# Five PSUM banks, later additions and one more one-hot buffer in the list stage of a two-layer relational graph convolution

## The chip, the core and the metric

The kernel runs on one core of a Trainium2 chip. The core has a matrix engine (TensorE, PE in the profile, with its weight loads as PEld), VectorE (DVE), ScalarE (ACT), GpSimd (POOL) and SyncE (SP), which issues transfers. The metric is the device time of one execution in microseconds (us). The kernel before takes 3114.19 us, the median of three runs (3112.14 to 3119.51).

## What is computed

A graph has N = 12500 nodes with C = 128 features and E = 200000 edges sorted by target `dst`. Each edge has one of ten relations, the greatest of ten of its attributes. Two layers follow each other:

```python
def _rgcn_layer(x, src, dst, edge_type, w_rel, root, bias):
    seg = dst * NUM_REL + edge_type
    xs = x[src]
    sums = segment_sum(xs, seg, num_segments=N * NUM_REL)
    cnt = segment_sum(ones(seg.shape), seg, num_segments=N * NUM_REL)
    mean = (sums / maximum(cnt, 1.0)[:, None]).reshape(N, NUM_REL, -1)
    return einsum('nrd,rdo->no', mean, w_rel) + x @ root + bias

h = relu(_rgcn_layer(x, src, dst, edge_type, w_rel1, root1, b1))
out = layernorm(x + _rgcn_layer(h, src, dst, edge_type, w_rel2, root2, b2))
```

All of it is float32.

## The kernel before

**Tiles.** The edges are cut into 1563 tiles of 128. A tile's source rows are fetched by one indirect transfer, which GpSimd issues (`gathered`, L751). A one-hot matrix, 128 edges by relations times target nodes, is made on VectorE by comparing each edge's key with a table of column numbers (`ones`, L759 to L771), and multiplied by the edge's weight 1/count on ScalarE (`weighted`, L757). TensorE multiplies rows by one-hot into a PSUM tile `zp`; VectorE adds `zp` into a ring `cc` of sums by relation and node, at an offset that it reads from memory into a register (`offsets`, L777, and `sum_into`, L792). When all edges of a block of nodes are in, TensorE multiplies its sums by the ten relation matrices (`projected`, L739 and L742), and the block is finished.

**Layer 1** (L832 to L1013) walks through all tiles in groups of four. A tile whose targets lie late enough finds many of its sources already finished; a table `XH` then holds both the input row and the row after layer 1, so one gather serves both layers, and the second layer's part is added to the second ring at once.

**Layer 2** (`layer_2`, L1289 to L1521) does what is left, in two kinds of bunches. First come 42 *plain* bunches, the first T0 = 166 tiles, four a bunch, with twelve node columns. Meanwhile `brought_together` (L1058) collects all other edges whose source was not finished in layer 1 into a dense *list* of 695 tiles, by shifting the edges of each of 127 rows together. That is long work on VectorE, cut into steps between the plain bunches. Then come 476 *list* bunches of one to three tiles, from two walks taken in turns: walk 0 over the first part of the list adds into ring 1, walk 1 into ring 0. A list tile's targets span w = 14 to 119 nodes; a bunch has 10 x w columns a tile and at most 512 in all. A tile of more than 48 columns is worked in pieces that begin at column c = 0, 48 and 96, each a bunch of its own, with one gather for all of them.

**Order.** The program's order on each engine is written out by hand. Step p of layer 2's loop (L1451 to L1516) issues:

- the one-hots of bunch p + 4 (AH = 4), on VectorE, and the weights of bunch p + 3, on ScalarE;
- the gathers of bunch p and its products, on TensorE (L1480);
- due jobs, such as the next step of `brought_together`;
- the additions of bunch p - 2 (BE = 2), on VectorE. A plain bunch whose first tile is a multiple of 128 first has its row of offsets loaded from `b_i` by a transfer on ScalarE's queue (L1504), and VectorE reads it from there;
- the projection of a block whose last bunch was just added, and later steps that are due (`turn`, `norm`, `cleared`).

An engine waits where its next instruction needs a buffer or a value that is not there; everything behind waits too.

**Buffers.** Gathered rows lie in 7 buffers of eight tiles, so GpSimd may be at most 56 tiles ahead. There are 6 one-hot buffers (`OB`). PSUM has eight banks of 512 float32 a partition: two for blocks and transposes (`ps_f`), three for products (`ps_y`), and three for one tile `mask` (`ps_m`, L1051), which holds scratch of `brought_together` and, at the end, the tables of column numbers that the one-hots compare with: twelve columns for plain tiles, and three tables for the list, one for each c (L1170 to L1174), made from `wide` (L1083). The block's tiles `xb`, `fT`, `a`, `v` and `o` hold 512 float32 a partition.

Of the kernel before, what the change touches and what calls it, by code (L numbers as in the profile page):

```python
# [20 lines left out]
P = 128  # L21
NREL = 10
# [9 lines left out]
GB = 7  # L32
OB = 6
GQ = 8
# [30 lines left out]
def rgcn_resnorm_kernel(ctx: ExitStack, tc: tile.TileContext, x, src, dst, attr, w_rel1, root1, b1,  # L65
# [572 lines left out]
    def rows_in(k):  # L638

        last = "e" if k == len(ranges[-1]) - 1 else ""  # L640
        xb = fin.tile([P, len(block(k)[2]) if last else 4, C], F32, name="xb" + last)
        rows_dma(xb, x, k, False)
        return xb

    def features_in(k, l, xb):

        n0, n, subs = block(k)
        last = "e" if k == len(ranges[-1]) - 1 else ""
        fT = fin.tile([P, (len(subs) if last else 4) * P], F32, name="fT" + last)
# [17 lines left out]
    def shifted(po, k, l):  # L667

        n = block(k)[1]
        tail = {NBLK - 1: "e", NBLK - 2: "d"}.get(k, "")  # L670
        a = fin.tile([P, P if tail else YB], F32, name="a" + tail)
        nc.scalar.activation(a[:, :n], po[:, :n], AF.Identity if l else AF.Relu, bias=bsb[l])  # L672
        return a
# [19 lines left out]
    def normed(k, xb, pr):  # L693

        v = fin.tile([P, 4, C], F32, name="v")
        mv = small.tile([P, 4, 2], F32, name="mv")
# [11 lines left out]
        o = fin.tile([P, 4, C], F32, name="o")  # L708
        for t, h in subs:
# [48 lines left out]

    def ones(keys, cols, n, w):  # L759

        oh = dpool.tile([P, YB], F32, name="oh")
        m = NREL * w
        o = oh[:, :n * m]
        if w == WN:
            nc.vector.tensor_tensor(o.rearrange("p (t m) -> p t m", m=m), cols[:, None, :m].to_broadcast([P, n, m]),  # L765
                                    keys[:, :, None].to_broadcast([P, n, m]), op=ALU.is_equal)
        else:
            nc.vector.tensor_tensor(o.rearrange("p (t r n) -> p t r n", r=NREL, n=w),  # L768
                                    cols[:, None, :, :w].to_broadcast([P, n, NREL, w]),
                                    keys[:, :, None, None].to_broadcast([P, n, NREL, w]), op=ALU.is_equal)  # L770
        return oh  # L771
# [60 lines left out]
    def layer_1():  # L832
# [6 lines left out]
        def finish(k, t):  # L839
# [39 lines left out]
            def second_kept(_):  # L879
                n0, n, _ = block(k)  # L880
                p2 = po.pop()
                t2 = fin.tile([P, YB], F32, name="v")
                nc.scalar.activation(t2[:, :n], p2[:, :n], AF.Identity, bias=bsb[1])  # L883
                nc.sync.dma_start(T2[:, n0:n0 + n], t2[:, :n])
# [18 lines left out]
            if k + 1 < NBLK - 1:  # L903
# [10 lines left out]
                def turned_kept(t):  # L914
                    n0, n, subs = block(k + 1)
                    pt = po.pop()
                    fTs[k + 1] = fin.tile([P, 4 * P], F32, name="fT")
                    nc.scalar.activation(fTs[k + 1][:, :n], pt[:, :n], AF.Copy)
# [139 lines left out]
    def brought_together(ready, first):  # L1058
# [15 lines left out]
        for to, a, o in ((Si, src, 0), (A[:, P:], CN, 0), (K, KD, L)):  # L1074
# [3 lines left out]
            if whole < NR:  # L1078
                nc.sync.dma_start(to[whole:NR, :real], bass.AP(a.tensor, a.offset + o + (NT - RT) * P, [[ER, 1], [1, real]]))
        tri, wide = flat[:, at:at + P], flat[:, at + P:at + P + NREL * WZ].rearrange("p (r n) -> p r n", n=WZ)  # L1080
        assert at + P + NREL * WZ <= NREL * RW
# [87 lines left out]
        yield 1  # L1169
        for c in range(0, WMAX, WZ):  # L1170
            w = min(WZ, WMAX - c)
            t = mask[:, c * NREL:(c + w) * NREL].bitcast(F32).rearrange("p (r n) -> p r n", n=w)
            nc.vector.tensor_scalar(t, wide[:, :, :w], float(c), None, op0=ALU.add)
            tables[c, WZ] = t  # L1174
        assert WMAX * NREL <= ER
        n = -(-NT2 // P)
# [4 lines left out]
        def put(i, c):  # L1181
# [4 lines left out]
            assert m * P <= EW  # L1186
            o = WMAX * NREL + i * (EW // P)
            assert o + EW // P <= EW - KW
# [100 lines left out]
    def layer_2():  # L1289
# [90 lines left out]
        def fetched(k):  # L1380
# [4 lines left out]
            if k != partial:  # L1385
                assert k != final or partial in ended
                xbs[k] = (comp if tail else fin).tile([P, 4, C], F32, name="xb" + tail)
                rows_dma(xbs[k], x, k, False)
            fTs[k] = (comp if tail else fin).tile([P, 4 * P], F32, name="fT" + tail)
            nc.sync.dma_start(fTs[k][:, :n], T2[:, n0:n0 + n])  # L1390

        def finish(k, i):
# [19 lines left out]
            def turn(_):  # L1412
                a = fin.tile([P, YB], F32, name="a")
                nc.scalar.activation(a[:, :n], po.pop()[:, :n], AF.Copy)
# [29 lines left out]
        gs, ohs, zps, offs = {}, {}, {}, {}  # L1444
        AH, BE = 4, 2
        i = 0
# [243 lines left out]
```

## Time and profile before

| | |
|---|---|
| median of three runs | 3114.19 us |
| the profiled execution, its own time | 3108.35 us |
| its span, first to last instruction | 3106.5 us |
| TensorE busy | 2368.2 us (76%), 11861 instructions |
| VectorE busy | 2031.1 us (65%), 5465 instructions |
| ScalarE busy | 1301.6 us (42%), 3177 instructions |
| GpSimd busy | 2295.8 us (74%), 2436 instructions |
| granted TensorE clock, mean of the span | 0.840 |

Positions are us from the span's start. Layer 2's gathers begin at 1969.4; the plain stage reaches to about 2210, the list stage from there to the end. In a group's row stand line, engine, operation, tile written <- tiles read, shapes and count, then busy time and mean ns of one, then idle time of the engine just before such instructions and what ended it. In the timeline stand start, duration, the instruction and in brackets the idle time before it with its releaser. "issue" is waiting that the profile cannot put down to anything. A busy share alone says little here: an engine can be in every slice the one that others wait for and still show gaps between its instructions.

### The profile page before, as it was taken

Reading aid. Unit: us, or ns where it says so; the run is one execution under the profiler, and the core shown is the slowest. Engines: PE = TensorE matmul, PEld = TensorE weight load, DVE = VectorE, ACT = ScalarE, POOL = GpSimd, SP = SyncE. Lnnn points to the kernel's source line nnn. Section 1 sums busy time; section 2 is a strip of 40 time slices with the busy share of each in tenths; the row PEclk is TensorE's granted clock in tenths of the full one; section 3 lists DMA queues with packets and bytes.
Section 4 is the critical chain, followed back from the end, with each engine's and each line's share of the span. In section 5 each row is a group of like instructions: output and inputs, shape, how many; then the busy total and the mean of one; then the engine's idle time right before and its main releaser. Section 6 shows DMA issues by size and latency. Waiting matters only on the chain.

```text
span 3106.5 us, 42362 instructions
## 1 busy us (share of the span) xinstructions
PE 2368.2 (76%) x11861; PEld 1949.5 (63%) x11861; DVE 2031.1 (65%) x5465; ACT 1301.6 (42%) x3177; POOL 2295.8 (74%) x2436
## 2 busy tenths in 40 slices
PE   2768787888787878787878788546467777777887
PEld 1556677777776767676767677545445555555665
DVE  6764657665656767655646464597776676777766
ACT  3533443433333434333433333332434455555643
POOL 7777777777777777777777777677777777777772
PEclk8768888888888889888888888767788888998988
DMA  6874444444545454545454444322222222222221
GB/s 191 270 216 143 141 145 141 140 146 122 161 122 162 124 157 129 159 122 160 125 158 127 128 121 118 95 59 62 64 67 68 72 73 74 72 73 73 79 73 43
DMA packets 265199, 370.97 MB, mean 119 GB/s; under 512 B 51232, under 2 KB 197189, under 8 KB 264958
## 3 DMA queue, kind: packets, MB, share of 16 engines
q0 software_dynamic: 99920, 250.57, 29.4%
q1 hardware_dynamic: 111347, 91.97, 9.4%
q10 hardware_dynamic: 53691, 25.62, 2.8%
q8 instruction: 102, 1.67, 0.2%
q14 instruction: 139, 1.14, 0.1%
HBM read 322.86 MB, written 57.89 MB: 123 GB/s over the span
## 4 chain that ended last, share of the span: by engine, by line
PE 30%; POOL 22%; issue 19%; DVE 14%; DMA 10%; ACT 2%; DVEq 1%; ACTq 0%; POOLq 0%; SPq 0%
POOL g L751 22%; PE pf L739 13%; DMA g<-XH,idxE 9%; PE zp L978 8%; PE zp L1480 6%; DVE cc L792 5%; DVE oh L768 2%; PE pf L742 1%; DVE cc L1158 1%; DVEq L777 1%; ACT cc L722 1%; ACT oh L757 1%; DVE oh L765 1%; DVE st L703 1%; DVE go L1146 1%
## 5 line engine op out<-in xcount | busy, mean ns | idle before, releaser
L751 POOL DMA_INDIRECT g<-XH,idxE x1397 | 1321.2, 946 | 425.6 <-issue 384.8
L792 DVE TENSOR_TENSOR cc<-cc,zp 128x240 f32 (+13 forms) x2500 | 959.8, 384 | 777.8 <-PE zp L978 388.2
L978 PE MATMUL zp<-oh,g 128*128 128x120 f32 x5920 | 983.2, 318 | 370.5 <-DMA g<-XH,idxE 206.8
L978 PEld LDWEIGHTS zp<-oh,g 128*128 128x128 f32 x5920 | 866.5, 222 | 487.2 <-issue 184.8
L751 POOL DMA_INDIRECT g<-hD,idxB x695 | 657.3, 946 | 215.9 <-issue 195.3
L739 PE MATMUL pf<-cc,w 128*128 128x256 f32 (+4 forms) x3000 | 732.1, 405 | 18.9 <-DVE cc L792 15.1
L1480 PE MATMUL zp<-oh,g 128*128 128x120 f32 (+23 forms) x1874 | 507.3, 415 | 284.4 <-DVE cc L792 156.4
L739 PEld LDWEIGHTS pf<-cc,w 128*128 128x128 f32 x3000 | 610.4, 215 | 121.1 <-DVE cc L792 22.5
L1480 PEld LDWEIGHTS zp<-oh,g 128*128 128x128 f32 x1874 | 338.9, 227 | 430.9 <-issue 271.0
L757 ACT ACTIVATE oh<-oh,wE 128x120 f32<-128x120 f32 x1729 | 530.9, 383 | 186.0 <-DVE oh L765 139.4
L757 ACT ACTIVATE oh<-oh,wB 128x150 f32<-128x150 f32 (+23 forms) x771 | 339.1, 482 | 296.5 <-DVE oh L768 269.4
L722 ACT ACTIVATE cc<-zero 128x1280 f32<-128x1280 f32 (+3 forms) x274 | 336.6, 1231 | 85.3 <-DVE cc L792 81.5
L768 DVE TENSOR_TENSOR oh<-go,keyB 128x480 f32<-128x480 f32 (+20 forms) x476 | 260.3, 547 | 115.1 <-PE zp L1480 113.6
L672 ACT ACTIVATE a<-pf,b 128x256 f32<-128x256 f32 (+1 forms) x50 | 23.3, 465 | 580.6 <-PE pf L742 578.9
L765 DVE TENSOR_TENSOR oh<-bank,keyE 128x480 f32<-128x480 f32 x391 | 253.0, 647 | 0.0
L751 POOL DMA_INDIRECT g<-hD,idxE x166 | 158.8, 957 | 61.7 <-issue 46.0
L751 POOL DMA_INDIRECT g<-in_x_dram,idxE x166 | 156.9, 945 | 52.2 <-issue 47.9
L883 ACT ACTIVATE v<-pf,b 128x256 f32<-128x256 f32 (+2 forms) x52 | 23.9, 459 | 361.4 <-PE pf L742 333.2
L548 DVE TENSOR_TENSOR eqb<-bank,kh 128x1344 bf16<-128x1344 f32 (+2 forms) x65 | 100.4, 1549 | 2.4 <-PE pf L559 2.0
L557 PE MATMUL pf<-eqb,identb 128*128 128x512 bf16 (+2 forms) x130 | 58.9, 453 | 12.4 <-DVE eqb L548 12.4
L559 PE MATMUL pf<-eqb,identb 128*128 128x512 bf16 (+2 forms) x130 | 58.5, 450 | 0.0
L706 ACT ACTIVATE rstd<-mv,eps 128x2 f32<-128x2 f32 (+5 forms) x54 | 15.9, 295 | 83.8 <-DVE mv L704 83.3
(235 smaller groups left out, 1097.8 us busy)
## 6 DMA issues: line engine op xcount, KB each, us to landing
m<-in_edge_attr_dram SPq DMA_DIRECT2D x48, 672.0 KB
g<-XH,idxE POOLq DMA_INDIRECT x1397
XH<-in_x_dram ACTq DMA_DIRECT2D x24, 512.0 KB
XH<-zero ACTq DMA_DIRECT2D x24, 512.0 KB
XH<-hb SPq DMA_DIRECT2D x87, 128.0 KB
g<-hD,idxB POOLq DMA_INDIRECT x695
xb<-in_x_dram SPq DMA_DIRECT2D x72, 128.0 KB
out_dram<-o SPq DMA_DIRECT2D x47, 128.0 KB
```

The source lines that it names most:

```text
L548: nc.vector.tensor_tensor(eq[:p], kpP[:p, None, :R].to_broadcast([p, DB, R]), fore, op=ALU.is_equal)
L557: nc.tensor.matmul(pc[:p], identb[:p, :p], eq[:p, k:k + 4, L:], start=(d + k == 1), stop=False)
L559: nc.tensor.matmul(pc[:p], identb[:p, :p], back, start=False, stop=(d + k + 3 == L))
L722: nc.scalar.activation(cc[:, l, h * H:(h + 1) * H, o:o + n], zero[:, None, :n].to_broadcast([P, H, n]), AF.Copy)
L739: nc.tensor.matmul(po[:, :n], wsb[l][:, r, :], cc[:, l if ring is None else ring, r, o:o + n], start=(r == 0), stop=False)
L751: nc.gpsimd.indirect_dma_start(out=g[:, j * C:(j + n) * C], out_offset=None, in_=table, in_offset=bass.IndirectOffsetOnAxis(ap=idx, axis=0))
L757: nc.scalar.activation(s, s, AF.Copy, scale=w)
L765: nc.vector.tensor_tensor(o.rearrange("p (t m) -> p t m", m=m), cols[:, None, :m].to_broadcast([P, n, m]), keys[:, :, None].to_broadcast([ ...
L768: nc.vector.tensor_tensor(o.rearrange("p (t r n) -> p t r n", r=NREL, n=w), cols[:, None, :, :w].to_broadcast([P, n, NREL, w]), keys[:, :, ...
L792: nc.vector.tensor_tensor(s, s, z, op=ALU.add)
L978: nc.tensor.matmul(zp[:, a + l * KW:a + (l + 1) * KW], g[:, (slot[j] + l) * C:(slot[j] + l + 1) * C], oh[:, j * KW:(j + 1) * KW], start=Tr ...
L1480: nc.tensor.matmul(zp[:, j * m:(j + 1) * m], gt[:, b * C:(b + 1) * C], oh[:, j * m:(j + 1) * m], start=True, stop=True)
```

## The change

Layer 2's list bunches get five PSUM banks in place of three. The tile `mask` is given back once the first list one-hots are due (`masking.close()` at p = plain - 4), and its three banks become the table `wide` and two product tiles `zq3` and `zq4`; bunch p takes one of `ps_y`'s three when p % 5 is 0, 1 or 2, and one of the two else. Only one table is left; a piece that begins at c = 48 or 96 adds c to it in the comparison. Additions come three bunches behind for list bunches, two for plain ones, as before. There are seven one-hot buffers, and the block's tiles shrink from 512 to 384 float32. The offsets of all plain tiles are loaded by two transfers on SyncE's queue when layer 2 begins, ahead of the loads of `brought_together`.

```diff
-OB = 6
+OB = 7
...
-        xb = fin.tile([P, len(block(k)[2]) if last else 4, C], F32, name="xb" + last)
+        xb = fin.tile([P, len(block(k)[2]) if last else 3, C], F32, name="xb" + last)
...
-    def ones(keys, cols, n, w):
+    def ones(keys, cols, n, w, c=0):
...
-            nc.vector.tensor_tensor(o.rearrange("p (t r n) -> p t r n", r=NREL, n=w),
-                                    cols[:, None, :, :w].to_broadcast([P, n, NREL, w]),
-                                    keys[:, :, None, None].to_broadcast([P, n, NREL, w]), op=ALU.is_equal)
+            to = o.rearrange("p (t r n) -> p t r n", r=NREL, n=w)
+            a = cols[:, None, :, :w].to_broadcast([P, n, NREL, w])
+            b = keys[:, :, None, None].to_broadcast([P, n, NREL, w])
+            if c:
+                assert n == 1
+                nc.vector.scalar_tensor_tensor(to[:, 0], a[:, 0], float(c), b[:, 0], op0=ALU.add, op1=ALU.is_equal)
+            else:
+                nc.vector.tensor_tensor(to, a, b, op=ALU.is_equal)
...
-    ps_m = fast.enter_context(tc.tile_pool(name="ps_m", bufs=1, space=PSUM))
     ps_y = fast.enter_context(tc.tile_pool(name="ps_y", bufs=3, space=PSUM))
+    masking = ExitStack()
+    ps_m = masking.enter_context(tc.tile_pool(name="ps_m", bufs=1, space=PSUM))
...
-        nc.vector.tensor_tensor(wide, spread[:, :, None].to_broadcast([P, NREL, WZ]),
-                                columns[:, None, :WZ].to_broadcast([P, NREL, WZ]), op=ALU.add)
...
-        for c in range(0, WMAX, WZ):
-            w = min(WZ, WMAX - c)
-            t = mask[:, c * NREL:(c + w) * NREL].bitcast(F32).rearrange("p (r n) -> p r n", n=w)
-            nc.vector.tensor_scalar(t, wide[:, :, :w], float(c), None, op0=ALU.add)
-            tables[c, WZ] = t
...
-        AH, BE = 4, 2
+        AH, BE = 4, 3
+        plain = sum(not b[1] for b in bunches)
+        rowP = comp.tile([1, -(-T0 // CT) * CT], I32, name="rowP")
+        for c in range(-(-T0 // CT)):
+            nc.sync.dma_start(rowP[:, c * CT:(c + 1) * CT], b_i[c:c + 1, :])
...
+            if p == plain - AH:
+                assert wanted[0] in ready
+                masking.close()
+                ps_n = fast.enter_context(tc.tile_pool(name="ps_n", bufs=1, space=PSUM))
+                tables[WZ] = ps_n.tile([P, NREL, WZ], F32, name="wide")
+                nc.vector.tensor_tensor(tables[WZ], spread[:, :, None].to_broadcast([P, NREL, WZ]),
+                                        columns[:, None, :WZ].to_broadcast([P, NREL, WZ]), op=ALU.add)
...
-                ohs[p + AH] = ones(keys[:, t0:t0 + n], tables[(c, WZ) if second else WN], n, w)
+                ohs[p + AH] = ones(keys[:, t0:t0 + n], tables[WZ if second else WN], n, w, c)
...
+            five = p >= plain
...
-                zp = zps[p] = ps_y.tile([P, YB], F32, name="zp")
+                if p % 5 > 2 and five:
+                    zp = ps_n.tile([P, YB], F32, name=f"zq{p % 5}")
+                else:
+                    zp = ps_y.tile([P, YB], F32, name="zp")
+                zps[p] = zp
...
-            q = p - BE
-            if q >= 0:
+            q = p - (BE if five else BE - 1)
+            if q in zps:
...
-                            if t % CT == 0:
-                                row = rows_.tile([1, CT], I32, name="row")
-                                nc.scalar.dma_start(row, b_i[t // CT:t // CT + 1, :])
-                            vals = offsets(row[:, t % CT:t % CT + m], t, m, bounds)
+                            vals = offsets(rowP[:, t:t + m], t, m, bounds)
```

More of the change, by code (lines that the diff above doesn't have):

```diff
@@ L648, in features_in @@
         last = "e" if k == len(ranges[-1]) - 1 else ""
-        fT = fin.tile([P, (len(subs) if last else 4) * P], F32, name="fT" + last)
+        fT = fin.tile([P, (len(subs) if last else 3) * P], F32, name="fT" + last)
         if l:
@@ L670, in shifted @@
         tail = {NBLK - 1: "e", NBLK - 2: "d"}.get(k, "")
-        a = fin.tile([P, P if tail else YB], F32, name="a" + tail)
+        a = fin.tile([P, P if tail else 3 * P], F32, name="a" + tail)
         nc.scalar.activation(a[:, :n], po[:, :n], AF.Identity if l else AF.Relu, bias=bsb[l])
@@ L693, in normed @@
     def normed(k, xb, pr):
-        v = fin.tile([P, 4, C], F32, name="v")
+        v = fin.tile([P, 3, C], F32, name="v")
         mv = small.tile([P, 4, 2], F32, name="mv")
@@ L707, in normed @@
             nc.vector.reciprocal(rstd[:p, s], rstd[:p, s])
-        o = fin.tile([P, 4, C], F32, name="o")
+        o = fin.tile([P, 3, C], F32, name="o")
         for t, h in subs:
@@ L881, in second_kept @@
                 p2 = po.pop()
-                t2 = fin.tile([P, YB], F32, name="v")
+                t2 = fin.tile([P, 3 * P], F32, name="v")
                 nc.scalar.activation(t2[:, :n], p2[:, :n], AF.Identity, bias=bsb[1])
@@ L916, in turned_kept @@
                     pt = po.pop()
-                    fTs[k + 1] = fin.tile([P, 4 * P], F32, name="fT")
+                    fTs[k + 1] = fin.tile([P, 3 * P], F32, name="fT")
                     nc.scalar.activation(fTs[k + 1][:, :n], pt[:, :n], AF.Copy)
@@ L1079, in brought_together @@
                 nc.sync.dma_start(to[whole:NR, :real], bass.AP(a.tensor, a.offset + o + (NT - RT) * P, [[ER, 1], [1, real]]))
[L1080 to L1081 removed]
+        tri = flat[:, at:at + P]
+        assert at + P <= NREL * RW
         yield 1
[L1083 to L1084 removed]
         nc.vector.memset(below, 1.0)
@@ L1186, in put @@
             assert m * P <= EW
-            o = WMAX * NREL + i * (EW // P)
+            o = i * (EW // P)
             assert o + EW // P <= EW - KW
@@ L1386, in fetched @@
                 assert k != final or partial in ended
-                xbs[k] = (comp if tail else fin).tile([P, 4, C], F32, name="xb" + tail)
+                xbs[k] = (comp if tail else fin).tile([P, 3, C], F32, name="xb" + tail)
                 rows_dma(xbs[k], x, k, False)
-            fTs[k] = (comp if tail else fin).tile([P, 4 * P], F32, name="fT" + tail)
+            fTs[k] = (comp if tail else fin).tile([P, 3 * P], F32, name="fT" + tail)
             nc.sync.dma_start(fTs[k][:, :n], T2[:, n0:n0 + n])
@@ L1412, in turn @@
             def turn(_):
-                a = fin.tile([P, YB], F32, name="a")
+                a = fin.tile([P, 3 * P], F32, name="a")
                 nc.scalar.activation(a[:, :n], po.pop()[:, :n], AF.Copy)
```

1 line of the change is left out of this document (removed).

## The prediction

> **What bounds the kernel now.** I read the page first, for the engine that is never idle for long.
>
> ```profile
> span 3106.5 us, 42362 instructions
> ...
> POOL 7777777777777777777777777677777777777772
> ...
> L751 POOL DMA_INDIRECT g<-hD,idxB x695 | 657.3, 946 | 215.9 <-issue 195.3 <-PE zp L1480 14.2 <-DMA g<-hD,idxB 4.3
> ```
>
> GpSimd issues one gather of 128 rows after another, in every slice but the last. Each takes 946 ns and has about 0.3 us of "issue" behind it. So I asked for the gathers of layer 2 alone, by stretches (length, busy time of GpSimd, number, clock, DMA), and then for the timeline.
>
> ```profile
> 1969.40:3051.90 1082.50, 816.18 (x861) 0.84 0.28 71
> ...
> 1969.40:2210.50 241.10, 182.84 (x192) 0.69 0.28 70
> 1969.40:2481.70 512.30, 387.31 (x408) 0.76 0.27 69
> ```
>
> ```profile
> 2210.54 1.74 PE L1480 MATMUL zp<-oh,g 128*128 128x140 f32 x6 [0.45 <-ACT oh L757]
> ...
> 2479.86 0.95 POOL L751 DMA_INDIRECT g<-hD,idxB  x1 [0.30 <-issue]
> 2482.81 0.94 POOL L751 DMA_INDIRECT g<-hD,idxB  x1 [2.01 <-PE zp L1480]
> ...
> 3050.91 0.94 POOL L751 DMA_INDIRECT g<-hD,idxB  x1 [0.30 <-issue]
> ```
>
> Undisturbed, a gather starts every 1.25 us (0.95 + 0.30). The 861 gathers of layer 2 took 1082.5 us, or 1.257 each, so GpSimd hardly ever stood still. It ended at 3050.91 + 0.94 = 3051.85, and the kernel 54.6 us later. Those 54.6 us are what a faster pipeline behind the gathers can win.
>
> How far the products lag can be counted. The first product of the list starts at 2210.54; 192 gathers were issued by then and 166 of them are plain tiles, so the lag is 26 tiles. At 2482.81 gather 409 waits for a product: 408 is 51 buffers of eight, the next needs the 45th back, hence tile 360 was just used, a lag of 48. The last tile's gather starts at 3050.91 and its product at 3089.70, 38.8 us or 31 tiles later. So from 2205 to 3085 compute is about as fast as the gathers and drags a backlog along, and the backlog is what is paid after 3051.85. What holds it back there, by the view of waits (who waited for whom: total, times, longest):
>
> ```profile
> PE zp L1480 <- DVE cc L792: 113.7, 66, 7.4
> DVE oh L768 <- PE zp L1480: 113.6, 46, 5.4
> PE zp L1480 <- issue: 45.9, 20, 4.1
> DVE cc L792 <- PE pf L739: 35.6, 7, 6.6
> POOL g L751 <- PE zp L1480: 13.9, 32, 2.3
> ```
>
> TensorE and VectorE wait for each other. A typical case from the timeline:
>
> ```profile
> 2617.92 4.50 PE L739 MATMUL pf<-cc,w 128*128 128x256 f32 x20
> 2619.69 0.26 DVE L792 TENSOR_TENSOR cc<-cc,zp 128x110 f32 x1
> ...
> 2622.68 1.99 PE L1480 MATMUL zp<-oh,g 128*128 128x160 f32 x10
> 2623.77 0.66 DVE L768 TENSOR_TENSOR oh<-go,keyB 128x480 f32<-128x480 f32 x1 [3.82 <-PE zp L1480]
> ```
>
> While TensorE projects a block (L739), VectorE finishes the two bunches it has, then wants the one-hot buffer of a product that stands behind the projection, and idles 3.82 us. Then TensorE in turn finds its three banks full.
>
> **The change, part by part.** *Five banks, additions three behind, seven one-hots.* With three banks product p needs the addition of p-3; with six one-hots, ones(p+4) needs product p-2. So three bunches are in flight. Afterwards product p needs the addition of p-5 and ones(p+4) product p-3: five in flight. At a projection VectorE has one bunch more to do, and TensorE may run two further ahead. What one bunch of VectorE is worth:
>
> ```profile
> L792 DVE TENSOR_TENSOR cc<-cc,zp 128x150 f32 (+22 forms) x787 | 308.3, 392 | 104.6 <-PE pf L739 35.6 <-issue 31.6 <-ACT cc L722 12.0
> ...
> L768 DVE TENSOR_TENSOR oh<-go,keyB 128x480 f32<-128x480 f32 (+24 forms) x474 | 259.2, 547 | 115.1 <-PE zp L1480 113.6
> ```
>
> 0.547 us for the one-hot and 787/474 x 0.392 = 0.65 us of additions, 1.2 us together. Over the 46 waits of VectorE that is at most 55 us of compute time. The lower bound is nothing: where the next addition goes to the ring that the projection reads, it waits for the projection itself (the 35.6 us above), whatever the banks. I take 45 to 55, since only 7 waits are of that kind.
>
> How much is needed? The first list product will start about 9 us earlier (below), near 2201.5, and gathers allow the last one near 3050. That is 848 us for the 695 tiles against 3090.3 - 2210.5 = 880 now, 32 us less. 32 of 45 to 55 is enough, so I expect compute to catch up before the end, and **the last gather to set the end**. Anything saved beyond that changes nothing.
>
> *Offsets of the plain tiles, loaded at once; tables.* The rows of the plain stage:
>
> ```profile
> 1993.17 0.91 DVE L792 TENSOR_TENSOR cc<-cc,zp 128x120 f32 x3 [5.42 <-DMA row<-b_i]
> ...
> 2131.99 1.80 DVE L1173 TENSOR_SCALAR go<-cc 128x480 f32<-128x480 f32 x3
> ...
> 2179.97 1.22 DVE L792 TENSOR_TENSOR cc<-cc,zp 128x120 f32 x4 [9.37 <-DMA row<-b_i]
> ...
> 2172.78 4.49 PE L1196 MATMUL pf<-cc 127*128 127x256 f32 x20
> 2181.30 1.34 PE L1480 MATMUL zp<-oh,g 128*128 128x120 f32 x8 [4.03 <-issue]
> ...
> 1975.89 0.38 SPq L1390 DMA_DIRECT2D fTe<-T  x1
> ...
> L777 DVEq TENSOR_LOAD <-row x21: 593/598/829, 1992.3 to 2213.7; - x21
> ```
>
> The first wait of 5.42 us shrinks to the register load of about 0.6: 4.8 won. Two loads more on SP, at 0.38 each by the row of another load there, push the list's source rows behind them back 0.8. Net 4.0. The three tables (1.80 us) go away while VectorE sets the pace, 1.8 won; one table comes back as one addition of 480 columns, 0.66 on VectorE at the end of the stage by the one-hot of that size above. The second row wait is 9.37 on VectorE, but TensorE was busy with L1196 until 2177.27 and then stood 4.03: 4.0 won. Sum 4.0 + 1.8 + 4.0 - 0.66 = 9 us, all of it backlog.
>
> *Shifted one-hots.* A list tile wider than 48 columns is worked in pieces. The 771 - 695 = 76 later pieces get their one-hot from one instruction with two operations in place of a plain comparison with a ready table:
>
> ```profile
> L757 ACT ACTIVATE oh<-oh,wB 128x150 f32<-128x150 f32 (+23 forms) x771 | 339.1, 482 | 296.5 <-DVE oh L768 269.4 <-PE zp L1480 12.0 <-DVE dn L1254 9.9
> ...
> L1192 DVE TENSOR_TENSOR cc<-columns,go 127x1536 f32<-127x1536 f32 x1 | 1.8, 1753 | 0.0
> L1168 DVE SCALAR_TENSOR_TENSOR cc<-cc 127x1536 f32<-127x1536 int32 x1 | 1.8, 1752 | 0.0
> ```
>
> Over 1536 columns both forms take 1.75 us, so I price it at nothing. The bound above is a second pass over the columns, 76 x 0.66 = 50 us of VectorE at most; no row suggests it.
>
> *Smaller tiles of the blocks* move nothing: no block here is wider than 280 columns, and 384 are left.
>
> **The sum**, against the profiled execution (span 3106.5, time 3108.35). GpSimd no longer waits for buffers: 13.9 - 32 x 0.30 = 4.3 us, so its last gather ends at 3047.6. The first gather of the layer waits for layer 1, which is untouched. Then:
>
> ```profile
> 2191.36 2.24 DMA g<-hD,idxB
> ```
>
> ```profile
> 3084.51 4.88 PE L739 MATMUL pf<-cc,w 128*128 128x280 f32 x20
> 3089.23 0.64 PE L742 MATMUL pf<-fT,ident 128*128 128x280 f32 x2
> 3089.70 0.58 PE L1480 MATMUL zp<-oh,g 128*128 128x250 f32 x2
> ...
> 3090.80 4.64 PE L739 MATMUL pf<-cc,w 128*128 128x260 f32 x20
> ```
>
> The chain has 2.24 us from the end of a gather to the work on its rows; with 2.3 the last ones are there at 3049.9. The last block but one is complete three bunches before the end, and its projection is issued one bunch later than now, so behind the last product: product 0.6, projection 3084.51 to 3089.87, 5.4, then 0.9 until the last projection, and from there to the end 3106.5 - 3090.8 = 15.7. Together 22.6, end at 3072.5, a gain of 34. I allow 1 us for a remaining lag: 33. The median of the runs (3114.19) lies 5.8 above the profiled one, so I forecast 3114 - 33 = **3081 us**, own range 3073 to 3092.
>
> **The rivals.** *Compute stays behind.* If additions after a projection mostly meet the ring that it reads, the third bunch of cover is not to be had, and only the 9 us and perhaps a third of the 45 remain: gain 9 to 24, 3090 to 3105, at 14 us 3100. For it: that wait exists (35.6 us), and grows as the others shrink. Against: 46 waits to 7.
>
> *TensorE becomes the bound, by its clock.* Once paced by gathers, TensorE has more gaps, and the granted clock may fall:
>
> ```profile
> 200.00:1950.00 1750.00, 1440.44 (x8018) 1247.61 (x8016) 1069.78 (x2841) 680.63 (x1768) 1323.48 (x1401) 0.85 0.48 139
> 2000.00:2150.00 150.00, 74.29 (x307) 63.39 (x307) 136.04 (x246) 40.12 (x113) 113.53 (x120) 0.62 0.23 59
> 2205.00:3085.00 880.00, 670.68 (x2631) 487.82 (x2630) 627.98 (x1791) 448.74 (x938) 637.50 (x674) 0.88 0.27 71
> ```
>
> The columns are TensorE, weight loads, VectorE, ScalarE and GpSimd, then the clock. TensorE is busy 670.7 us of the list stage at 0.88. Of its 209 us idle, 113.7 + 45.9 are the ones in question, about 50 stay. At clock c it needs 670.7 x 0.88/c + 50, more than today's 880 below c = 0.71. The stage of 2000 to 2150 ran at 0.62 with TensorE half idle, so this is possible; at 0.68 the stage takes 918, 38 more than now, less the 9 gained before: 3143 us, slower. Against it: layer 1 is paced by gathers all along and holds 0.85.
> The Trainium skill, "TensorE: Matmul & The Clock Gate", section "A second HAM failure mode: psum-queue depth-cycling", speaks for this rival: a kernel that cycled through PSUM banks idled TensorE briefly between groups often enough that the clock swung between half and full. The 0.62 of that stage agrees with it, the 0.85 of layer 1 does not.
>
> *The change does not do what it says*: the two-operation one-hot costs its second pass, up to 50 us on VectorE, and eats the 45 to 55. Then 3105 to 3118, no change to speak of.
>
> **How the numbers follow.** Forecast 0.70, compute stays behind 0.19, second pass 0.04, clock 0.07. The range, 3073 to 3104, takes the forecast's own range and nearly all of the first rival; what is outside is the last two and some of the edges. A measurement here tells 0.2%, 6 us, from no change. Faster: 0.70 + 0.18 = 0.88; same 0.05; slower 0.07.
>
> **What would show it.** Right: the last gather starts near 3047 and no wait of GpSimd for a product is over 0.5 us; TensorE's waits for gathers appear among the list's products, and the wait on L792 falls under half of 113.7; the last product comes within 3 us of the last landing; no row load waits on VectorE. Wrong: a product of the last tile over 10 us behind its gather (compute stays behind: look for L792 waiting on L739), a clock under 0.75 in the list stage, or a one-hot of 480 columns with two operations at over 0.8 us.

## The result and the profile after

| | before | after |
|---|---|---|
| median of the runs beside each other | 3113.22 us (3110.39 to 3119.51) | 3086.33 us (3084.58 to 3086.88) |
| ratio, 95% interval | | 0.991 (0.9895 to 0.9924) |
| span of the profiled execution | 3106.5 us | 3084.8 us |
| granted TensorE clock, mean of the span | 0.840 | 0.834 |

The change makes the kernel 27 us faster. Forecast was 3081 us, with a range of 3073 to 3104. First the gathers of layer 2 in the changed kernel, in one stretch (length, busy time of GpSimd, number, clock, DMA share, GB/s):

```profile
1970.00:3048.90 1078.90, 816.72 (x861) 0.83 0.28 73
```

Then GpSimd's waits from 1969 to 3060 (who waited for whom: total, times, longest):

```profile
POOL g L751 <- PE pf L742: 12.6, 3, 12.0
POOL g L751 <- PE zp L1494: 7.0, 23, 0.3
...
POOL g L751 <- PE zq L1494: 1.8, 6, 0.3
```

Apart from the 12.0 us at the layer's first gather (11.4 before), no wait for a product is longer than 0.3 us, where the longest was 2.3. The full ring is gone. The last gather ends at 3048.87 (its row is in the timeline below), against 3051.85, though the first began 0.6 us later.

TensorE's and VectorE's waits in the list stage, 2195 to 3065:

```profile
DVE cc L797 <- PE pf L739: 48.4, 9, 10.1
PE zp L1494 <- DVE cc L797: 43.5, 24, 9.0
...
DVE oh L775 <- PE zp L1494: 34.1, 15, 5.9
DVE oh L775 <- PE zq L1494: 28.7, 11, 5.8
PE pf L739 <- DVE cc L797: 28.2, 16, 5.6
...
PE zq L1494 <- DVE cc L797: 21.4, 15, 3.8
...
DVE oh L773 <- PE zp L1494: 13.2, 7, 3.9
```

L1494 is the product of before's L1480, L797 the addition (L792), L775 the one-hot (L768), L773 the one-hot of a later piece. In the same window of the kernel before, TensorE waits 122.9 us for additions that free a bank and VectorE 110.0 us for products; after, these are 64.9 (zp and zq together) and about 77 (with L773). From 2205 to 3085, the window of the prediction's rows, TensorE's went from 113.7 to 55.9. The waits of additions for a projection that reads their ring grew from 35.6 to 48.4, and projections now wait 28.2 us for additions (7.2 before).

What ends the waits of TensorE late in the list, 2700 to 3053, after and then before:

```profile
PE zp L1494 <- DMA g<-hD,idxB: 14.6, 23, 1.5
PE zq L1494 <- DVE cc L797: 12.9, 9, 2.7
PE zq L1494 <- DMA g<-hD,idxB: 10.5, 16, 1.4
```

```profile
PE zp L1480 <- DVE cc L792: 33.3, 27, 3.4
...
PE zp L1480 <- DMA g<-hD,idxB: 2.4, 2, 1.8
```

Products now wait for rows (25.1 us, 39 times), before they hardly did (2.4). The backlog can be counted at any product: gathers begun by then, less the tiles of the bunches ahead of it. Each cell gives tiles and the position in us; "run" is from bunch 48 to bunch 324, all list bunches. The last three rows are experiments told below.

| kernel | bunch 48 | bunch 180 | bunch 324 | bunch 480 | run |
|---|---|---|---|---|---|
| before | 29 at 2236.7 | 49 at 2481.7 | 41 at 2730.1 | 31 at 3005.3 | 493.4 |
| after | 19 at 2224.5 | 37 at 2465.9 | 9 at 2685.4 | 5 at 2968.5 | 460.9 |
| banks alone | 28 at 2234.1 | 49 at 2479.9 | 34 at 2716.5 | 16 at 2982.3 | 482.4 |
| before, fewer additions | 29 at 2237.9 | 49 at 2482.3 | 30 at 2714.2 | 4 at 2969.5 | 476.3 |
| after, fewer additions | 19 at 2224.1 | 38 at 2465.8 | 8 at 2684.1 | 5 at 2968.1 | 460.0 |

The changed kernel runs 32.5 us faster between bunches 48 and 324 and stands 2 to 14 tiles behind the gathers from then on. So the backlog of 31 tiles is gone, and yet the span is only 21.7 us shorter. The rest was given back at the end. The timeline of the changed kernel from its last gather (start, duration, instruction, in brackets the idle time before it with its releaser):

```profile
3044.72 0.87 SPq L634 DMA_DIRECT2D out_dram<-o  x2
...
3047.93 0.94 POOL L751 DMA_INDIRECT g<-hD,idxB  x1 [0.30 <-issue]
...
3052.94 1.17 PE L1494 MATMUL zp<-oh,g 128*128 128x250 f32 x2 [0.46 <-DMA g<-hD,idxB]
...
3053.90 6.21 PE L739 MATMUL pf<-cc,w 128*128 128x280 f32 x20
...
3061.72 0.61 DVE L700 TENSOR_TENSOR v<-pf,xb 128x256 f32<-128x256 f32 x2 [11.48 <-PE pf L1419]
...
3063.99 0.85 DVE L710 TENSOR_SCALAR o<-v,mv,rstd 128x128 f32<-128x128 f32 x3
...
3064.76 2.31 DVE L797 TENSOR_TENSOR cc<-cc,zp 128x250 f32 x5
3067.13 6.16 PE L739 MATMUL pf<-cc,w 128*128 128x260 f32 x20 [5.45 <-DVE cc L797]
```

VectorE stands idle 11.48 us until the last block but one has been projected and turned round, normalizes it (L700 to L710), and only then adds the last five tiles, which the last projection waits for. TensorE stands 5.45 us. Both projections are also longer than before's (4.88 and 4.64). The windows of the two projections with the clock (length, then busy time and count of TensorE, weight loads, VectorE, ScalarE, GpSimd, then clock, DMA share, GB/s), after and before:

```profile
3053.90:3060.10 6.20, 6.20 (x22) 4.84 (x21) 0.00 (x0) 0.00 (x0) 0.00 (x0) 0.78 0.00 0
...
3067.10:3073.30 6.20, 6.17 (x21) 5.16 (x22) 0.00 (x0) 0.00 (x0) 0.00 (x0) 0.75 0.01 3
```

```profile
3084.51:3089.30 4.79, 4.79 (x22) 3.88 (x21) 1.06 (x3) 0.00 (x0) 0.00 (x0) 1.00 0.02 3
3090.80:3095.40 4.60, 4.60 (x23) 4.02 (x22) 2.81 (x13) 0.59 (x2) 0.00 (x0) 1.00 0.12 33
```

### The profile page after: what moved, and what is told of

Its sections match the earlier page's. It is cut to its first block, busy times and chain, and to the rows that moved or that the text cites. A ratio compares the mean times of both kernels' runs of the same rounds, so it can differ in the third digit from the quotient of the medians.

```text
span 3084.8 us, 42354 instructions
## 1 busy us (share of the span) xinstructions
PE 2376.9 (77%) x11861; PEld 1961.6 (64%) x11861; DVE 2025.7 (66%) x5462; ACT 1299.9 (42%) x3177; POOL 2296.4 (74%) x2436
## 4 chain that ended last, share of the span: by engine, by line
PE 29%; POOL 21%; issue 18%; DVE 15%; DMA 12%; ACT 2%; DVEq 1%; ACTq 0%; SPq 0%; POOLq 0%
POOL g L751 21%; PE pf L739 14%; PE zp L983 10%; DMA g<-XH,idxE 9%; DVE cc L797 5%; DVE oh L775 2%; PE zp L1494 1%; DMA g<-hD,idxB 1%; PE pf L742 1%; DVE cc L1162 1%; PE zq L1494 1%; DVE oh L765 1%; DMA g<-in_x_dram,idxE 1%; DVEq L782 1%; DVE go L1150 1%
## 5 line engine op out<-in xcount | busy, mean ns | idle before, releaser
L797 DVE TENSOR_TENSOR cc<-cc,zp 128x240 f32 (+11 forms) x2193 | 839.8, 383 | 704.4 <-PE zp L983 392.4
L983 PE MATMUL zp<-oh,g 128*128 128x120 f32 x5920 | 995.3, 321 | 362.5 <-DMA g<-XH,idxE 210.3
L983 PEld LDWEIGHTS zp<-oh,g 128*128 128x128 f32 x5920 | 877.7, 225 | 481.4 <-issue 177.7
L739 PE MATMUL pf<-cc,w 128*128 128x256 f32 (+4 forms) x3000 | 747.4, 411 | 59.5 <-DVE cc L797 41.1
L739 PEld LDWEIGHTS pf<-cc,w 128*128 128x128 f32 x3000 | 620.1, 218 | 170.2 <-DVE cc L797 52.4
L1494 PE MATMUL zp<-oh,g 128*128 128x120 f32 (+20 forms) x1260 | 329.6, 402 | 148.7 <-DVE cc L797 77.2
L1494 PEld LDWEIGHTS zp<-oh,g 128*128 128x128 f32 x1260 | 224.5, 227 | 224.9 <-issue 123.7
L775 DVE TENSOR_TENSOR oh<-wide,keyB 128x480 f32<-128x480 f32 (+17 forms) x400 | 229.3, 573 | 63.1 <-PE zp L1494 34.1
L1494 PE MATMUL zq<-oh,g 128*128 128x160 f32 (+21 forms) x614 | 174.7, 412 | 61.8 <-DVE cc L797 21.4
L1494 PEld LDWEIGHTS zq<-oh,g 128*128 128x128 f32 x614 | 109.3, 213 | 114.1 <-issue 63.0
L797 DVE TENSOR_TENSOR cc<-cc,zq 128x160 f32 (+21 forms) x307 | 119.6, 390 | 55.1 <-PE pf L739 32.7
```

Of the source, the lines that this page charges most:

```text
L739: nc.tensor.matmul(po[:, :n], wsb[l][:, r, :], cc[:, l if ring is None else ring, r, o:o + n], start=(r == 0), stop=False)
L775: nc.vector.tensor_tensor(to, a, b, op=ALU.is_equal)
L797: nc.vector.tensor_tensor(s, s, z, op=ALU.add)
L983: nc.tensor.matmul(zp[:, a + l * KW:a + (l + 1) * KW], g[:, (slot[j] + l) * C:(slot[j] + l + 1) * C], oh[:, j * KW:(j + 1) * KW], start=Tr ...
L1494: nc.tensor.matmul(zp[:, j * m:(j + 1) * m], gt[:, b * C:(b + 1) * C], oh[:, j * m:(j + 1) * m], start=True, stop=True)
```

## The experiments

Three sets of four kernels ran, each set on one chip beside the kernel before. The chips were not alike: the kernel before took 4048.33 us in the first set, 3109.58 in the second and 4002.80 in the third. Ratios are to the kernel before of the same set.

**The norm put off again.** In `finish` the time to put a block's turn and norm off is 0 once no gather is left to come (`i < NG`). With additions three bunches behind, the last block but one is finished in just that state. The edit puts it off whenever another block is still due:

```diff
-            u = (1 if n > YB * 5 // 8 else 0.7) if i < NG else 0
+            u = (1 if n > YB * 5 // 8 else 0.7) if i < NG or due else 0
```

> The changed kernel with the norm of block 25 put off again, behind the last additions, on a chip where the kernel before takes about 3113 us. Theory (in the changed kernel's trace the norm of block 25 stood ahead of the last five additions and kept the last projection waiting 5.45 us): 4 to 6 us faster than the changed kernel, 3080 to 3083 us, ratio to the kernel before 0.9893 to 0.9905. Rival (the norm then only moves behind the last projection and is waited for at the end instead): no gain, 3085 to 3087 us, ratio 0.991. Where the kernel before takes about 4050 us again: 0.991 as in the run before.

3079.52 us (3077.69 to 3080.07), ratio 0.990 (0.9885 to 0.9915), span 3077.3. Timeline of its end:

```profile
3052.43 1.17 PE L1494 MATMUL zp<-oh,g 128*128 128x250 f32 x2 [0.54 <-DMA g<-hD,idxB]
...
3053.39 6.02 PE L739 MATMUL pf<-cc,w 128*128 128x280 f32 x20
3053.64 0.42 DVE L797 TENSOR_TENSOR cc<-cc,zp 128x250 f32 x1 [0.85 <-PE zp L1494]
...
3060.82 4.55 PE L739 MATMUL pf<-cc,w 128*128 128x260 f32 x20
3061.02 0.61 DVE L700 TENSOR_TENSOR v<-pf,xb 128x256 f32<-128x256 f32 x2 [6.97 <-PE pf L1419]
```

The last addition is over before the first projection has well begun, the last projection follows without a wait, and it takes 4.55 us in place of 6.16. From the last product to the end it is 24.9 us (3077.3 - 3052.43) in place of 31.9. That is 7.0 us, slightly more than the 4 to 6 expected, since the clock came back with the wait gone. The rival falls. By its median and its span this version is the fastest that computes everything. Its ratio's interval overlaps that of the changed kernel, which ran elsewhere; in its own set the changed kernel with fewer additions, told below, has the old end and took 3085.95 us.

In the first set, on a chip where all took some 900 us longer:

> The changed kernel with one edit in finish: the steps of the last block but one (transposes, normalisation) are put off, as they were before the change, until the last block is finished; in the changed kernel they come at once, ahead of the last three additions. Theory (order on VectorE): the last projection of the changed kernel starts at 3067.1, 5.45 us after TensorE is free, because the additions stand behind a normalisation that waits for the projection before; with the edit it starts near 3061.7 and the kernel takes 5 us less than the changed one, about 3081 us, ratio to the kernel before 0.989 to 0.990. Rival (the additions wait for the projection's reading of the ring anyway, so the normalisation is hidden): no change, 3086 us, 0.991.

4000.0 us, ratio 0.991 (0.9886 to 0.9934). That is the ratio of this expectation's rival, but the changed kernel did not run in that set, and without it the ratio says nothing about the edit.

**The banks alone.** Five banks, but six one-hots and additions two bunches behind; the early loads and the single table stay:

```diff
-OB = 7
+OB = 6
...
-            q = p - (BE if five else BE - 1)
+            q = p - (BE - 1)
```

> Five banks in tiles of their own, one-hots in six buffers, additions two bunches behind. Theory (each of the three parts gives some of the time that the products gain on the gathers): it comes out between the two kernels, 3090 to 3100 us, ratio 0.9925 to 0.996; the last gather ends within 3 us of the changed kernel's 3048.9 us, and products stand 10 to 25 tiles behind it there. Rival (the banks alone do it): products have caught up with the gathers before the last one and the ratio is 0.990 to 0.9915.

3098.52 us, ratio 0.9968 (0.9956 to 0.998), span 3093.9. The time lies in the theory's range, the ratio just above its 0.996. The timeline's last gather and last product:

```profile
3046.97 0.94 POOL L751 DMA_INDIRECT g<-hD,idxB  x1 [0.30 <-issue]
...
3076.97 0.58 PE L1494 MATMUL zp<-oh,g 128*128 128x250 f32 x2
```

The gathers end at 3047.91, a little earlier than with the whole change, but the last product comes 29 us behind. By the table above the banks alone give 11.0 of the 32.5 us between bunches 48 and 324. The rival, that they do it by themselves, falls. On the chip of the first set:

> The changed kernel with five banks, but additions two behind and six one-hot buffers. Theory (at a projection it is VectorE that runs out of work first): VectorE still has two bunches only, its wait for products stays over 90 us in the list stage, TensorE's wait for additions falls; compute gains less than half: the last product 5 to 25 us after its gather, 3090 to 3100 us, ratio 0.992 to 0.996. Rival (free banks are all that counts): as the changed kernel or, since the last steps come in the old order, 3080 to 3086 us, 0.989 to 0.991.

4045.72 us, ratio 1.0002 (0.9987 to 1.0017): no gain in time there.

**Is it VectorE's chain?** The 76 additions of later pieces are left out, in the kernel before and in the changed one:

```diff
-                    sum_into(slice(ring, ring + 1), zps[q], j * NREL * w, offs[second, t], w, c)
+                    if not c:
+                        sum_into(slice(ring, ring + 1), zps[q], j * NREL * w, offs[second, t], w, c)
```

> The kernel before, with the 76 additions of pieces from column 48 on left out (about 35 us of VectorE's time in the list stage). Theory (before the change the chain product, addition, free bank sets the pace of the list stage, and its products still stand 31 tiles behind the gathers at the last one): 15 to 25 us faster than the kernel before, ratio 0.992 to 0.995. Rival (something other than VectorE's chain holds the products back, TensorE's own work or the gathers' landing): under 6 us faster, ratio 0.998 to 1.000.

> The changed kernel with the same 76 additions left out (about 35 us of VectorE's time). Theory (after the change the gathers alone set the time of the last product, so VectorE's time in the list stage is free): 0 to 4 us faster than the changed kernel, 3082 to 3087 us, ratio to the kernel before 0.990 to 0.9915; the last gather ends at the same time. Rival (VectorE's chain still sets the pace): 20 us or more faster than the changed kernel, ratio 0.985 or less.

The kernel before becomes 31.4 us faster: 3078.16 us, ratio 0.9898 (0.9883 to 0.9913), span 3075.0. The changed kernel does not move: 3085.95 us, ratio 0.9919 (0.9904 to 0.9934, just above the 0.9915 expected), span 3084.3. What was taken out shows in the windows of all additions from 2195 to 3095 (length, VectorE's busy time in them, number, clock), of the kernel before and of this version of it:

```profile
2195.00:3095.00 900.00, 310.29 (x793) 0.88 0.27 70
```

```profile
2195.00:3095.00 900.00, 280.48 (x717) 0.87 0.27 70
```

The 76 additions are 29.8 us, not the 35 of the expectation. So the same work is worth its whole price before the change and nothing after it. The edit takes out more than VectorE's time, though: the banks of these 76 products also come free without an addition. From bunch 48 to bunch 480 the kernel before runs 36.9 us faster with it, and how much of this is VectorE's time and how much the earlier banks was not tried. The end of the kernel before with fewer additions:

```profile
3049.25 0.94 POOL L751 DMA_INDIRECT g<-hD,idxB  x1 [0.30 <-issue]
...
3052.78 4.88 PE L739 MATMUL pf<-cc,w 128*128 128x280 f32 x20
...
3057.96 0.58 PE L1480 MATMUL zp<-oh,g 128*128 128x250 f32 x2
...
3059.06 4.64 PE L739 MATMUL pf<-cc,w 128*128 128x260 f32 x20
```

Its backlog runs down to 4 tiles at bunch 480, with three banks. It gained more than the 15 to 25 expected: the whole piece, since the backlog is used up altogether. With additions two behind, the projection of the last block but one goes ahead of the last product, runs while the last rows land, and meets a clock of 1.00:

```profile
3052.78:3057.66 4.88, 4.88 (x22) 3.96 (x21) 0.83 (x2) 0.00 (x0) 0.00 (x0) 1.00 0.00 0
```

**The other parts, one at a time.** The two early loads put into the kernel before:

```diff
+        rowP = comp.tile([1, -(-T0 // CT) * CT], I32, name="rowP")
+        for c in range(-(-T0 // CT)):
+            nc.sync.dma_start(rowP[:, c * CT:(c + 1) * CT], b_i[c:c + 1, :])
...
-                            vals = offsets(row[:, t % CT:t % CT + m], t, m, bounds)
+                            vals = offsets(rowP[:, t:t + m], t, m, bounds)
```

> The kernel before with the plain tiles' offsets loaded at once and nothing else. Theory (before, the end is set by compute that lags behind the gathers): the second row's wait of 9.37 us on VectorE goes, the list starts 7 to 8 us earlier and so does the end: 3105 us, ratio 0.997 to 0.998; the first row's wait goes too but gains nothing, since the products of that place wait for gathers. Rival (the lag at the list's start is made up or lost again later): no change, 3113 us.

> The kernel before with the two early loads of the plain tiles' offsets alone. Theory (the loads' wait stood in VectorE's chain, and what is saved in the plain stage reaches the list's products, which set the end): 3 to 9 us faster, ratio 0.997 to 0.999. Rival (it is hidden by the chain of the list stage): ratio 0.9995 to 1.0005.

Then the changed kernel with three banks and additions two behind, keeping seven one-hots, the single table and the early loads:

```diff
-            five = p >= plain
+            five = False
```

> The changed kernel with three banks for all bunches and additions two behind; one-hot buffers, the single table and the loads stay as changed. Theory (banks and distance give the speed): compute stays behind the gathers, GpSimd waits again for products with a full ring of buffers, the last product comes over 20 us after its gather; only the earlier start of the list is left: 3100 to 3105 us, ratio 0.996 to 0.9975. Rival (the seventh one-hot buffer and the loads do it): 3086 to 3090 us.

> Three banks, additions two behind as before the change, but seven one-hot buffers, the single table and the two early loads of the plain tiles' offsets. Theory (without the banks the chain product, addition, free bank still sets the pace; only the earlier start of about 8 to 12 us at the list's first bunches is left, and part of it is lost to the same chain): 3098 to 3108 us where the kernel before takes 3110 us, ratio 0.996 to 0.9995. Rival (buffers and loads are the change, the banks nothing): ratio 0.990 to 0.992.

The changed kernel with six one-hots:

```diff
-OB = 7
+OB = 6
```

> The changed kernel with six one-hot buffers in the place of seven (five banks, additions three behind). Theory (with additions three bunches behind, a seventh one-hot lets the comparison run ahead by as many bunches as before; with six it waits for the product of a bunch nearer): it falls between the changed kernel and the one with the banks alone, 3087 to 3097 us on a chip where the kernel before takes 3110 us, ratio 0.9925 to 0.996. Rival (the seventh buffer does nothing): as the changed kernel, ratio 0.990 to 0.992.

and the changed kernel as it is, beside them:

> The changed kernel once more, beside the others on one chip, so that they can be compared with it: 3083 to 3087 us where the kernel before takes 3110 to 3113 us, ratio 0.990 to 0.9925. Theory and rival agree on it; a ratio outside this would mean that chips differ by more than the experiments do.

All these ran on the slower chips, so the positions and times that their expectations state for a normal one were not put to the test. What they gave, with the time from bunch 48 to bunch 480 counted in each trace:

| set | kernel | ratio, 95% interval | bunch 48 to 480, us |
|---|---|---|---|
| first | early loads alone | 1.0026 (1.0009 to 1.0043) | 998.4 |
| first | three banks | 1.0002 (0.9985 to 1.0019) | 995.3 |
| first | banks alone | 1.0002 (0.9987 to 1.0017) | 977.9 |
| first | norm put off | 0.991 (0.9886 to 0.9934) | 942.7 |
| third | early loads alone | 0.9999 (0.9983 to 1.0015) | 980.5 |
| third | three banks | 0.9964 (0.9947 to 0.998) | 975.5 |
| third | six one-hots | 1.002 (1.0003 to 1.0037) | 988.2 |
| third | changed kernel | 0.9956 (0.994 to 0.9971) | 938.9 |

The early loads alone and the three banks each came out 0.27% and 0.38% apart in the two sets, so a difference under some 0.4% says nothing on these chips. Part of it lies ahead of layer 2: in the third set's three versions of the changed kernel, whose layer 1 is the same, the first gather of layer 2 starts between 2549.9 and 2555.3. A gain of the early loads was not to be seen, the three banks stayed far from their rival's 0.990 to 0.992, and six one-hots came out level with the kernel before, which neither theory nor rival had. The changed kernel's own 0.9956, in place of 0.991, lies outside its expectation: the change is worth less on this chip. The stretch of the list says more. There products stand 39 to 55 tiles behind and GpSimd waits for them, as in the early loads' kernel over its whole run ("remote" is a releaser that the profile does not name):

```profile
POOL g L751 <- PE zp L1483: 238.2, 57, 12.5
POOL g L751 <- remote: 229.1, 82, 10.7
```

So compute sets the pace to the end, and the stretch measures compute. Five banks alone win 20 us of it against the early loads alone, three banks with seven one-hots 3 to 5. Five banks with additions three behind but six one-hots lose 8. All parts together win 42 and 56 (the latter with the norm put off, which changes nothing before the last blocks). Each stretch is one trace, and where it begins matters: counted from the first list bunch, 42, the same differences are 18 us won, 3 to 5 won, none, and 49 and 63 won. So a loss with six one-hots is not shown, only that in this trace the five banks and the third bunch of cover bring nothing without the seventh buffer; and 42 to 63 are far more than any part gave. The three belong together. A likely reason, argued and not tested: with six one-hots VectorE waits at step p for product p-2 before its comparison, and the addition behind it on the queue is now that of bunch p-3, which was ready earlier. Its bank comes free later.

## Why the prediction was right, and where its sizes were off

**What bounds before, and what bounds after** was right. The two runs with fewer additions settle it: 76 additions less, 29.8 us of VectorE's work and as many waits for a bank, are worth 31.4 us before and nothing after. The forecast had compute catching up; the 32 us that it needed were there (12.2 us ahead at bunch 48 and 32.5 more by bunch 324). The wait that the rival "compute stays behind" named grew as it said, from 35.6 to 48.4 us, but did not hold compute back. TensorE's waits for additions were to fall under half of 113.7, which is 56.9, and fell to 55.9 in that window: the sign came, barely. Catching up did not need the rest of the 45 to 55 us, and the estimate cannot be told right or wrong beyond what was used. On the two slower chips, where compute stays behind to the end, the 42 and 56 us are near it, but the waits there are others.

**The early loads and the tables** brought less than priced. The first list product, bunch 42, was to start 9 us earlier, near 2201.5. It starts at 2207.7, 2.8 us earlier. At the first row VectorE won nothing of the 4.0. The timeline of VectorE there, after:

```profile
1995.16 0.66 DVE L765 TENSOR_TENSOR oh<-go,keyE 128x480 f32<-128x480 f32 x1 [6.56 <-PE go L1115]
```

It waits 6.56 us for TensorE in place of 5.42 for the row, since TensorE's products ahead of L1115 wait for gathers:

```profile
1984.64 0.78 PE L1494 MATMUL zp<-oh,g 128*128 128x120 f32 x2 [2.60 <-DMA g<-hD,idxE]
```

Bunch 24 starts at 2105.5 as before (2105.4). At bunch 36 the changed kernel is 9.6 us ahead, and then loses most of it. ScalarE clears a ring for the list (L1209), and a block's copy (L1412), which VectorE waits for through TensorE, stands behind that:

```profile
2175.45 4.25 ACT L1209 ACTIVATE cc<-zero 128x512 f32<-128x512 f32 x8
...
2189.39 0.37 ACT L1412 ACTIVATE a<-pf 128x256 f32<-128x256 f32 x1
...
2190.54 0.42 DVE L700 TENSOR_TENSOR v<-pf,xb 128x256 f32<-128x256 f32 x1 [14.14 <-PE pf L1419]
```

VectorE stands 14.14 us there, where it stood 4.70 in the kernel before: what it had won it now waits for ScalarE, and the sum of the forecast had no such wait. At bunch 48 the changed kernel is 12.2 us ahead, so 9.4 us are won in the six bunches from 42 on. The banks alone have 4.0 at bunch 42 and 2.6 at bunch 48, so this gain hangs on the third bunch of cover and the seventh one-hot, at the step from plain to list bunches, which I had not priced. That the forecast's 9 us lie near these 12.2 is luck.

**The one-hot with two operations at no price** was right. One-hots of 480 columns in the changed kernel, with one operation and with two:

```profile
L775 DVE TENSOR_TENSOR oh<-wide,keyB 128x480 f32<-128x480 f32 x92 | 59.5, 647 | 4.7 <-PE zp L1494 2.5 <-PE zq L1494 2.3
...
L773 DVE SCALAR_TENSOR_TENSOR oh<-wide,keyB 128x480 f32<-128x480 f32 x18 | 11.7, 650 | 6.5 <-PE zp L1494 6.5
```

**TensorE's clock as the bound** fell as a rival for the list. Windows of the changed kernel's list stage, columns as in those of the projections:

```profile
2205.00:2690.00 485.00, 369.95 (x1471) 269.87 (x1471) 362.15 (x1080) 257.28 (x533) 366.89 (x388) 0.87 0.28 73
2700.00:3030.00 330.00, 268.54 (x1043) 198.86 (x1043) 237.97 (x643) 177.15 (x375) 249.84 (x263) 0.88 0.29 75
```

The clock stayed at 0.87 and 0.88 (before, in the same windows, 0.86 and 0.91), far from the 0.71 from which it would have decided. It came back small, at the very end.

**The end is the term that was mis-sized.** I summed 22.6 us from the last landing to the end and an end at 3072.5 without the 1 us for lag. It was 3084.8, 12.3 later, term by term:

| term | forecast | measured | difference |
|---|---|---|---|
| end of the last gather | 3047.6 | 3048.87 | +1.3 |
| from there to its product | 2.3 | 3052.94 - 3048.87 = 4.07 | +1.8 |
| product to projection | 0.6 | 3053.90 - 3052.94 = 0.96 | +0.4 |
| first projection to its last matmul | 5.4 | 3060.59 - 3053.90 = 6.69 | +1.3 |
| from there to the last projection | 0.9 | 3067.13 - 3060.59 = 6.54 | +5.6 |
| last projection to the end | 15.7 | 3084.8 - 3067.13 = 17.67 | +2.0 |

(3060.59 is the end of the matmul that closes the projection, 3059.95 + 0.64.) The step that failed is the one that moved the projection by one bunch and nothing else. Additions three behind move `finish` of the last block but one past the last gather. There it no longer puts its norm off, and the norm goes in front of the last additions. The run with that one line changed gives back 7.0 us of the 12.3. Of the rest, 0.6 is the later first gather. The longer first projection is not mended by it (6.02 us at a clock of 0.81).

In the median the miss is 5.3 us, not 12.3 less 1: I added the 5.8 us by which before's median lay above its profile, and the changed kernel's median (3086.33) lies on its profiled time (3086.65). That this addition hid about half of the miss is luck.

## What to carry to other kernels

A seemingly local depth (additions two or three behind) also decides which side of an "any work left?" test the last iterations fall on: step through the last three by hand, in issue order on each engine. To tell whether an engine's chain sets the pace, take a known piece of its work out in both versions. A gain of the piece's size, or none, answers it, but look what else the piece frees (here the banks). Depths that feed each other (banks, distance of the additions, one-hot buffers) should be tried together: the banks alone gave a third of what all of them gave between bunches 48 and 324 (11.0 of 32.5 us).

## What was not expected of the hardware

**The clock of a projection depends on the few microseconds before it.** The same 20 matmuls of 260 columns took 4.64 us before, 6.16 after a wait of 5.45 us (clock 0.75), and 4.55 when that wait was taken away. Those of 280 columns took 4.88 at 1.00, and 6.21 at 0.78 and 6.02 at 0.81 where products ahead had waited singly for rows. The window of the last, with the norm put off:

```profile
3053.40:3059.40 6.00, 6.00 (x22) 4.68 (x21) 0.42 (x1) 0.00 (x0) 0.00 (x0) 0.81 0.00 0
```

The Trainium skill, "TensorE: Matmul & The Clock Gate", section "What's actually happening", has the clock at half after an idle window of about 3.4 us and full again after a busy one. The trace agrees in kind: in the changed kernel's two last projections the clock is 0.50 for the first 2.7 us (3053.90 to 3056.57) and the first 3.1 us (3067.10 to 3070.23), and 1.00 from there to the end of each. With 3.1 of 6.2 us at half, the mean is the 0.75 of the row.

**Landings were slower at the end.** The last gather's product began 4.07 us behind the gather in the changed kernel, 4.26 with the norm put off (3052.43 - 3048.17), against the 2.24 us of the prediction's row. Earlier in the changed kernel's list, from 2700 to 3030, the 35 products that waited for their rows began 1.55 to 2.51 us behind the gather, 1.69 in the median. SyncE issued output and input transfers at 3044.7 to 3047.3, as the row above begins to show, and the DMA engines' busy share was 0.60 from 3044 to 3049 where it was 0.29 from 2700 to 3030. That these transfers are the cause was not tried. SyncE issues such transfers in mid-list too. For 8 of the 35 products it had issued one since 4 us before the end of their gather, and they too began within 2.13 us of it.

**Chips differ by more than the change.** On two of the chips all kernels took 29 to 30% longer, at a granted clock of 0.75 to 0.77 in place of 0.83 to 0.84. Their gathers took 948 ns as elsewhere (946 before), as a group of the early loads' kernel from 2700 to 3000 shows:

```profile
L751 POOL DMA_INDIRECT g<-hD,idxB x114 | 108.0, 948 | 105.8 <-PE zp L1483 36.9 <-issue 29.6 <-DVE vB L1262 23.2
```

What grew are waits that the profile can't put down to anything. The kernel before, and the early loads' kernel in the third set, over the whole run:

```profile
PEld zp L978 <- issue: 184.8, 123, 18.8
```

```profile
PEld zp L978 <- issue: 716.3, 538, 24.0
...
DVE cc L792 <- remote: 577.2, 101, 16.1
```

What stands behind them stays open, and so does whether the lower clock is a cause or a consequence.
